# Attention and quantized feed-forward on one core: a new list of work (24 steps written out, the loop, the last eight), results summed into x, the norm as (x + minus) * rstd

## The chip, the cores and the metric

The kernel runs on 1 core of a Trainium2 chip. Its engines work side by side, each from a queue of its own, in order: TensorE (PE, with its weight loads shown as PEld), VectorE (DVE), ScalarE (ACT), GpSimd (POOL) and SyncE (SP), which here issues every DMA. The metric is the device time in microseconds (us); lower is better.

## The reference, cut to what matters

`x` has 4 batches of 2048 rows of 512 numbers, so 64 tiles of 128 rows.

```
x = x + (attention(layernorm(x), context) @ Wout + bout)
h = layernorm(x) * gamma + beta
h = qlinear(h, w1, b1)        # 512 -> 2048
h = gelu(h)
x = x + qlinear(h, w2, b2)    # 2048 -> 512

def qlinear(x, w, b):
    scale_x = 127 / max(abs(x), per row);  xq = round(x * scale_x)
    scale_w = 1 / mean(abs(w));            wq = clip(round(w * scale_w), -1, 1)
    return xq @ wq.T / (scale_x * scale_w) + b
```

The attention's mask lets query i see key j only where j mod 2048 equals i. A batch has 154 keys, so each of the first 154 queries of a batch sees one key and the result is that key's value row; every other query sees no key, all its scores are equal, and the result is the mean of the value rows. So the attention is a table of rows per batch: 128 rows (`front`), a tile of 26 rows and 102 times the mean (`second`), and the mean (`mean`), each multiplied by Wv and Wout.

## The kernel before, in words

The whole kernel is one list of short words, which `do` turns into instructions in exactly that order (`manual_schedule`). Each engine's queue is the part of the list that it executes; nothing else orders the work. `BEGINNING` is written out for the setup and steps U0 to U11, `STEADY` holds four steps with relative numbers and is repeated for rows 12 to 55, and `ENDING` holds the last eight. A step begins with `U`, the up product of row tile n. `n` counts row tiles in the order of `seq`, which puts a batch's first two tiles last.

Setup: `lv`, `lo` load Wv and Wout, `w` multiplies one block of them on TensorE (eight blocks, L415); `lw` loads a 1024-wide chunk of w1 (`lw0`) or w2 (`lw1`) into a buffer of the pool `ring`; `ms` sums its absolute values (L228 on DVE, L234 on ACT); `z0`, `z1` make the weight's scale (three parts: DVE, a small TensorE product of the tile `tot` at L206, DVE); `q` rounds the chunk (L217, L219) and `c` clips it (L222). `lc` loads the context, `lr0` to `lr3` load bout, gamma, beta and b2, `lb` half of b1. `pm`, `pr`, `Y` are TensorE products (L444) for the mean, the second tiles and the front tiles of a batch; `sr` writes the rows of the second tiles to DRAM, and `s`, `t` spread them from there with DMAs (`s`: L493 for 26 rows and L496 for the mean row repeated over 102 partitions; `t`: L499).

For each row tile: `L` loads a pair of tiles of x into a `ring` buffer. `a` (POOL) or `A` (DVE) adds the attention row (L246). `S` (DVE) takes mean and variance (L253). `N` (POOL, eight small instructions, L269 to L276), or `O`, `o`, `C` for the first four groups, makes rstd of a group of one to four tiles. The normed tile h is made by `k` (POOL, L306) or `n` (ACT, L299), followed by `e` (POOL: times gamma L311, plus beta L312); or by `P` and `E` on DVE alone (L320: (x - mean) * gamma; L325: times rstd, plus beta). `R` (DVE, L334) takes the largest value of a row; the group's last `R` makes the scale; `V` (POOL) or `v` (DVE) makes two more scales of the group. `Q` (ACT, L354) rounds h into 16-bit numbers and `T` transposes them by DMA (L365) into xqT, the operand of `U`. `X` (POOL) or `x` (DVE) adds b2 to x (L328).

`I n.half.v` seeds one half of the up product's PSUM tile with b1 times a scale (v = 1: DVE L524, v = 0: ACT L526). There are three such halves for all steps. `U` (16 products, L534) adds to it. `G` (ACT, L553) is the gelu of a half, `M` (DVE, L565) its largest value, the second `M` also makes the scale; `H` (ACT, L594) rounds the hidden row, `h` transposes it by DMA (L605) into hqT, and `W` (16 products, L612) is the down product into one of two PSUM tiles. `D` (POOL, L587) makes its scale, `F` (DVE, L618) computes x plus the scaled product into a tile `o` of two buffers, and `f` stores it (L623).

In the loop, `W` runs two steps behind `U`, loads run 14 to 16 tiles ahead, and behind the groups of rows that start at 12, 28 and 44 an `s`, behind the one that starts at 24 a `t` is inserted.

Of the kernel before, what the change touches and what calls it, by code (L numbers as in the profile page):

```python
# [37 lines left out]
F32 = mybir.dt.float32  # L38
I16 = mybir.dt.int16
# [14 lines left out]
def xattn_ffn(ctx: ExitStack, tc, x, ctxT, WvT, Wout, bout, w1T, b1, w2T, b2, gamma, beta, out):  # L54
# [22 lines left out]
    for g, size in enumerate(sizes):  # L77
# [4 lines left out]
    FIRST = 12  # L82
    BEGINNING = """
        lv0 lo0 lo1 lo2 lv1 lw0.2 lw0.3 lw0.6 lv2 w0 lw0.0 lv3 lv4 lo3 ms0.2.1 lo4 w1
        ms0.3.0 lw0.7 ms0.6.0 lw0.1 lo5 w2 ms0.0.1 lv5 lw0.4 lo6 lw0.5 lv6 w3 ms0.7.0 lo7
        ms0.1.1 lv7 lc w4 lw1.4 ms0.4.0 lw1.6 L0 ms0.5.0 lr0 w5 lr1 z0.0 lw1.2 z0.1 w6
        z0.2 q0.0.1 q0.5.0 q0.2.1 lw1.0 q0.7.0 lw1.5 sk2 c0.2.0 L1 sk3 c0.5.0 q0.4.0 sk1
        w7 lw1.3 ms1.4.0 sk0 c0.4.0 lw1.7 c0.7.0 cw0.1 q0.1.0 sf c0.0.0 cw1.0 lw1.1 pm0.2
        lr2 cw3.1 cw2.0 lk q0.3.0 c0.1.1 mk pm2.4 xo1 ms1.6.0 L2 q0.6.1 c0.6.1 L3 ms1.2.0
        Y0.0.2 m lb0 A0 a1 ms1.5.0 S0 Y0.2.4 ms1.0.0 O0 P0 o0 a2 ms1.3.0 C0 pr0.2 S1  # L90
        ms1.7.0 a3 O1 y0 ms1.1.0 c0.3.0 S2 o1 E0 a5 z1.0 R0 z1.1 z1.2 Q0 O2 Y3.0.2 P1 o2
        q1.6.0 T0 a6 C2 q1.2.0 L4 C1 lb1 V0 lr3 q1.0.0 E1 c1.2.0 Y3.2.4 R1 I0.0.0 P2 V1
        q1.3.0 pr2.4 a4 y3 S3 Q1 a8 I0.1.0 T1
        U0 O3 S4 L5 L6 c1.6.0 q1.7.0 S5 o3 E2 end G0.0 c1.0.0 C3 I1.0.0 R2 a7 I1.1.0
        U1 M0.0 V2 Q2 N4 P3 G0.1 c1.3.1 E3 q1.5.0 Y2.0.2 yr k4 q1.4.0 R3 k5 sr L7 e4 T2
        q1.1.0 Y2.2.4 S6 I2.0.1 G1.0 Y1.0.2 c1.1.0 G1.1 S7 M0.1 V3 I2.1.0 a10
        U2 I3.0.0 a13 M1.0 Q3 H0 M1.1 e5 T3 L8 s0 Y1.2.4 R4 G2.0 h0 N6 P6 L9 H1 A9 c1.7.1
        c1.5.1 R5 X0 I3.1.0
        U3 h1 t1 y1 G2.1 V4 M2.0 k7 I4.0.0 X3 S13 Q4 c1.4.0 W0 M2.1 G3.0 T4 a12 L10 G3.1
        S8 a11 Q5 y2 I4.1.0 T5 a14 M3.0  # L100
        U4 I5.0.0 e7 S9 H2 M3.1 W1 N8 G4.0 E6 h2 A15 G4.1 R6 R7 D0 I5.1.0 X1
        U5 M4.0 H3 D1 k8 F0 X4 S10 n9 D2 V6 Q6 S11 e8 W2 I6.0.0 T6 F1 h3 M4.1 G5.0 f0
        I6.1.0 X2 S12
        U6 H4 e9 S14 R8 Q7 M5.0 G5.1 T7 X5 R9 W3 f1 h4 G6.0 D3 N10 I7.0.1 Q8 A19 I7.1.0 T8
        M5.1 L11 V8 Q9
        U7 k10 G6.1 T9 a16 F2 n11 I8.0.1 f2 e10 H5 F3 W4 M6.0 G7.0 h5 a20 S16 n12 a17 M6.1
        I8.1.0
        U8 e11 G7.1 M7.0 I9.0.0 R10 H6 e12 R11 W5 M7.1 G8.0 h6 f3 D6 x7 D7 I9.1.0 D5 a18
        R12
        U9 H7 S15 D4 X6 F4 Q10 S17 a21 G8.1 T10 M8.0 W6 f4 V10 h7 G9.0 X10 S20 I10.0.0  # L110
        M8.1 N13 I10.1.0
        U10 S18 H8 k13 F5 k15 M9.0 X8 G9.1 h8 F6 e13 W7 Q11 S19 Q12 T11 M9.1 f5 G10.0 L12
        T12 N16 I11.0.0 f6 A22 W8 H9 x9 S21 a23 M10.0 I11.1.0 h9 D9 e15 S22 G10.1
        U11 F7 I12.0.0 M10.1 f7 D8 G11.0 k14 e14 W9 M11.0 H10 F8 k16 R13 I12.1.0 h10 e16
        R14 G11.1 R15 n17 M11.1 n18 e17 Q13 R16 H11 T13 F9 f8 V13 R17 f9 D10 X11 h11 t2
        e18
    """
# [21 lines left out]
    ring = ctx.enter_context(tc.tile_pool(name="ring", bufs=12))  # L139
# [99 lines left out]
    stats, rstd, shift, scale1, deq1, inv1 = {}, {}, {}, {}, {}, {}  # L239
# [24 lines left out]
    def row_norms(g):  # L264
# [3 lines left out]
        shift[g] = small.tile([P, 4], F32, tag="shift", name=f"shift_{g}")[:, :size]  # L268
# [353 lines left out]
    def store(n):  # L622
        nc.sync.dma_start(out=out_tiles[:, seq[n], :], in_=rows_out.pop(n))  # L623
# [131 lines left out]
```

## Time and profile before

| | |
|---|---|
| median of 3 runs | 524.63 us (524.53 to 524.99) |
| the profiled execution | 525.17 us, span 523.2 us |
| PE, DVE, ACT, POOL busy | 501.1, 433.2, 426.3, 410.5 us |
| DMA queue of SyncE | 93.56 MB, 75.1% of 16 engines |

A line of a timeline gives start, duration, engine, line, operation, output <- inputs and count, and in brackets the engine's idle time ahead of it and what ended it. A line of the groups gives count, then busy us and mean ns of one, then the idle time before the group. "x16" beside a product counts TensorE instructions; consecutive products overlap, so the distance from start to start (3.453 us for a `U` or a `W`) is the time they take. "PEclk" is the granted TensorE clock in tenths. In SyncE's timeline a DMA's duration is the time that the issuing took, not the transfer.

### The profile page before, as it was taken

To read this page: it belongs to the slowest core of one execution; us is meant where nothing else is said; L and a number is where in the kernel's file an instruction comes from. 1 tells how busy PE (TensorE), PEld (TensorE's weight loads), DVE (VectorE), ACT (ScalarE), POOL (GpSimd) and SP (SyncE) were. 2 spreads that over 40 slices of the span, in tenths; PEclk is the share of its full clock that TensorE was granted. 3 is DMA by queue.
4 is the path that set the end of the run, shared out by engine and by line. 5 is a ranking of instruction groups with operands and counts; after the bars stand their busy time and mean duration, and the time that the engine had idled before them with its cause. 6 is when DMAs were issued, how large, how long until landed. Compare 5 with 4: busy or idle time off the path is not lost.

```text
span 523.2 us, 6893 instructions
## 1 busy us (share of the span) xinstructions
PE 501.1 (96%) x2168; PEld 223.8 (43%) x2168; DVE 433.2 (83%) x753; ACT 426.3 (81%) x393; POOL 410.5 (78%) x532
## 2 busy tenths in 40 slices
PE   8997987999999989999999989999999899999996
PEld 3443432444444434444444434444444344444442
DVE  0188999889799889899999988999999888787762
ACT  2278987999788879888888878888889798888971
POOL 0048999999999999899999898999999998852220
PEclk9997998999999999999999999999999999999999
DMA  8998569376979695858697987679586956575664
GB/s 289 399 391 306 188 132 200 84 178 137 195 161 221 141 199 139 201 137 201 149 205 160 178 183 180 164 164 198 133 203 128 201 112 147 110 166 132 135 112 125
DMA packets 194112, 94.00 MB, mean 180 GB/s; under 512 B 170268, under 2 KB 170268, under 8 KB 194076
## 3 DMA queue, kind: packets, MB, share of 16 engines
q1 hardware_dynamic: 194076, 93.56, 75.1%
q8 instruction: 17, 0.28, 0.2%
q14 instruction: 19, 0.16, 0.1%
HBM read 34.55 MB, written 17.04 MB: 99 GB/s over the span
## 4 chain that ended last, share of the span: by engine, by line
PE 57%; POOL 18%; DMA 10%; DVE 6%; ACT 4%; issue 3%; SPq 1%; DVEq 0%; ACTq 0%; POOLq 0%
PE ph L534 27%; PE po L612 26%; DMA xqT<-xqg 6%; PE wps L415 4%; POOL x L246 4%; POOL h L312 3%; POOL h L311 3%; DVE m L565 2%; POOL x L328 2%; DMA x<-x_dram 2%; ACT hq L594 2%; DMA wv<-WvT_dram 2%; POOL h L306 1%; POOL r L270 1%; ACT hid L553 1%
## 5 line engine op out<-in xcount | busy, mean ns | idle before, releaser
L534 PE MATMUL ph<-w1q,xqT 128*128 128x512 f16 x1024 | 233.4, 381 | 10.1 <-DMA xqT<-xqg 7.8
L612 PE MATMUL po<-w2q,hqT 128*128 128x512 f16 x1024 | 231.3, 379 | 1.9 <-DMA hqT<-hq 1.2
L565 DVE TENSOR_REDUCE m<-hid 128x1 f32<-128x1024 f32 (+1 forms) x130 | 153.1, 1192 | 27.0 <-ACT hid L553 26.6
L553 ACT ACTIVATE hid<-ph,d 128x1024 f32<-128x1024 f32 (+1 forms) x130 | 140.9, 1095 | 31.4 <-PE ph L534 30.1
L534 PEld LDWEIGHTS <-xqT 128*128 128x128 f16 x1024 | 100.0, 98 | 135.2 <-DMA xqT<-xqg 12.1
L612 PEld LDWEIGHTS <-hqT 128*128 128x128 f16 x1024 | 100.0, 98 | 123.4 <-DMA hqT<-hq 2.2
L594 ACT ACTIVATE hq<-hid,i 128x2048 f16<-128x2048 f32 (+1 forms) x65 | 128.2, 1974 | 28.3 <-ACT ph L526 10.2
L526 ACT ACTIVATE ph<-b_b,inv 128x1024 f32<-128x1024 f32 x86 | 95.3, 1112 | 3.2 <-POOL inv L348 2.1
L312 POOL TENSOR_TENSOR h<-h,beta_b 128x512 f32<-128x512 f32 x59 | 75.6, 1282 | 4.6
L311 POOL TENSOR_TENSOR h<-h,gamma_b 128x512 f32<-128x512 f32 x59 | 75.0, 1271 | 3.9
L328 POOL TENSOR_TENSOR x<-x,b_b 128x512 f32<-128x512 f32 x61 | 77.0, 1272 | 0.0
L246 POOL TENSOR_TENSOR x<-x,mean 128x512 f32<-128x512 f32 x52 | 65.7, 1273 | 5.0 <-DVE mean L661 3.8
L618 DVE SCALAR_TENSOR_TENSOR o<-po,d,x 128x512 f32<-128x512 f32 x64 | 47.8, 746 | 16.0 <-PE po L612 10.6
L524 DVE TENSOR_SCALAR ph<-b_b,inv 128x1024 f32<-128x1024 f32 x42 | 53.2, 1267 | 0.6 <-ACT hid L553 0.6
L334 DVE TENSOR_REDUCE m<-h 128x1 f32<-128x512 f32 x64 | 42.9, 673 | 5.0 <-POOL h L312 5.0
L354 ACT ACTIVATE xqg<-h,s 128x512 f16<-128x512 f32 x64 | 45.4, 712 | 1.6 <-DVE s L342 1.6
L587 POOL TENSOR_TENSOR d<-mh,wm 128x1 f32<-128x1 f32 x64 | 12.5, 206 | 41.2 <-DVE mh L580 37.4
L253 DVE BATCH_NORM_STATS2 bn<-x 128x6 f32<-128x512 f32 x64 | 43.4, 679 | 0.6 <-POOL x L246 0.6
L306 POOL TENSOR_SCALAR h<-x,rstd,shift 128x512 f32<-128x512 f32 x54 | 41.9, 776 | 0.2
L415 PE MATMUL wps<-wo,wv 128*128 128x512 f32 x64 | 28.1, 595 | 1.5 <-DMA wv<-WvT_dram 1.5
L222 POOL TENSOR_SCALAR w1q<-wi 128x1024 f16<-128x1024 int16 x6 | 6.3, 1070 | 27.7 <-DVE wi L217 27.5
L415 PEld LDWEIGHTS wps<-wo,wv 128*128 128x128 f32 x64 | 11.9, 190 | 17.3 <-issue 13.9
(76 smaller groups left out, 261.3 us busy)
## 6 DMA issues: line engine op xcount, KB each, us to landing
x<-x_dram SPq DMA_DIRECT2D x32, 512.0 KB, 4.2
out_dram<-o SPq DMA_DIRECT2D x64, 256.0 KB, 2.8
ws<-w1T_dram SPq DMA_DIRECT2D x8, 512.0 KB, 7.2
ws<-w2T_dram SPq DMA_DIRECT2D x8, 512.0 KB, 9.6
wv<-WvT_dram SPq DMA_DIRECT2D x8, 256.0 KB, 8.5
wo<-Wout_dram SPq DMA_DIRECT2D x8, 256.0 KB, 4.5
ctx_sb<-ctxT_dram SPq DMA_DIRECT2D x1, 1232.0 KB
hqT<-hq SPq DMA_TRANSPOSE x65, 4.3
```

The lines of the kernel that those rows point to most:

```text
L246: e.tensor_tensor(x_of(n), x_of(n), y, ALU.add)
L311: nc.gpsimd.tensor_tensor(normed[n], normed[n], gamma_b, ALU.mult)
L312: nc.gpsimd.tensor_tensor(normed[n], normed[n], beta_b, ALU.add)
L328: e.tensor_tensor(x_of(n), x_of(n), b2_b, ALU.add)
L415: nc.tensor.matmul(wps[k // 2][:, (k % 2) * 512 : (k % 2 + 1) * 512], wv[c][:, k * P : (k + 1) * P], wo[c], start=(c == 0), stop=(c == KI ...
L524: nc.vector.tensor_scalar(ph, row, d, None, ALU.mult)
L526: nc.scalar.activation(ph, row, AF.Identity, bias=0.0, scale=d)
L534: nc.tensor.matmul(bank[i], xqT[n][:, k, :], w1q[:, k, i * 512 : (i + 1) * 512], start=False, stop=(k == KD - 1), skip_group_check=True,)
L553: nc.scalar.activation(hidden[n][:, i * w : (i + 1) * w], up_ps[n][half][:, lo : lo + w], AF.Gelu, bias=0.0, scale=deq1[g][:, j : j + 1],)
L565: nc.vector.tensor_reduce(m2[:, i : i + 1], hidden[n][:, i * w : (i + 1) * w], AX.X, ALU.max, apply_absolute_value=True,)
L594: nc.scalar.activation(hq[n][:, lo : lo + w], hidden[n][:, lo : lo + w], AF.Identity, bias=0.0, scale=inv2[n],)
L612: nc.tensor.matmul(po, hqT[n][:, k, :], w2q[:, k, :], start=(k == 0), stop=(k == KH - 1))
```

## The change

The list is replaced as a whole: `BEGINNING` now runs to step U23, the loop covers rows 24 to 55, and the last eight have another order. Words of each kind, before and after: `e` 59, 50; `k` 54, 50; `n` 5, none; `g` (new) none, 7; `P` 5, 14; `E` 5, 7; `X` 61, 59; `x` 3, 5; `V` 9, 12; `v` 12, 9; seeds on DVE 42, 37 and on ACT 86, 91; `ms` on DVE 3, 7 and on ACT 13, 9; `q` on DVE 3, 2 and on ACT 13, 14. All other counts stay, loads, transposes, stores, products and the four `s` and three `t` among them.

`F` writes its result over x, and `f` stores it from there, so tile `o` is gone and `ring` has 13 buffers for 12. `N` makes `minus` = -mean in place of `shift` = -mean * rstd, one instruction less. `k` computes (x + minus) * rstd. The new word `g` ends what `P` began on POOL: times rstd, plus beta.

```diff
-    FIRST = 12
+    FIRST = 24
...
+        lv0 lo0 lo1 lv1 lw0.5 lv2 lo2 lw0.7 lw0.3 w0 lw0.0 lo3 lo4 lv3 lw0.6 lv4 lw0.1 w1
+        lw0.4 ms0.0.0 lw0.2 lv5 ms0.7.0 lw1.5 lo5 w2 ms0.6.0 lc lo6 ms0.1.1 lv6 w3 ms0.3.1
+        lv7 ms0.4.1 lw1.7 L0 ms0.2.1 w4 lo7 ms0.5.1 lw1.2 z0.0 z0.1 w5 z0.2 ms1.5.1 q0.5.0
+        lr1 lw1.3 q0.3.0 sk1 lr0 q0.6.1 lw1.1 q0.0.0 c0.3.0 sk3 w6 sk2 L1 c0.5.0 q0.1.0
+        sk0 lw1.0 ms1.7.0 c0.1.1 mk lw1.6 sf q0.4.1 q0.2.0 w7 lw1.4 c0.2.1 L2 c0.4.1
+        q0.7.0 lr2 cw0.0 c0.7.0 L3 cw1.0 c0.0.0 pm0.2 cw2.1 ms1.2.0 lb0 lk xo0 cw3.1 pm2.4
+        ms1.1.1 lb1 c0.6.0 ms1.0.0 Y0.0.2 m A0 a1 ms1.6.0 S0 Y0.2.4 O0 ms1.4.0 P0 o0 a2 S1
+        ms1.3.0 C0 a3 S2 E0 a5 z1.0 R0 z1.1 z1.2 Q0 a6 O1 pr0.2 y0 q1.5.0 T0 V0 P2 lr3 L4
+        o1 I0.0.0 P1 L5 a7 C1 I0.1.0 O2 E1
+        U0 q1.1.0 o2 a4 S3 q1.4.0 O3 R1 c1.1.0 q1.6.0 S4 o3 q1.0.0 V1 c1.5.1 Y3.0.2 C2 X0
+        Q1 C3 end G0.0 T1 a9 pr2.4 S5 L6 I1.0.0 c1.6.1 N4 P3 q1.2.0 Y3.2.4 E2 I1.1.0 yr
+        U1 k5 R2 q1.3.0 E3 V2 G0.1 k4 M0.0 G1.0 a8 y3 Y1.0.2 I2.0.0 R3 c1.2.0 Q2 M0.1 e5
+        Y1.2.4 G1.1 T2 sr Q3 S8 Y2.0.2 I2.1.0 T3 S6 e4 y1 q1.7.0
+        U2 M1.0 H0 V3 R4 c1.7.0 S7 G2.0 h0 c1.3.0 R5 t1 Y2.2.4 I3.0.0 M1.1 c1.4.0 I3.1.0
+        c1.0.0
+        U3 S9 Q4 V4 N6 P6 H1 T4 A12 A11 G2.1 h1 W0 x3 N8 L7 E6 I4.0.0 L8 A10 G3.0 y2 k7
+        M2.0 I4.1.0
...
+        U16 k23 I17.0.1 X14 h14 G16.0 M15.1 f7 D14 X13 W13 G16.1 e23 F12 Q18 M16.0 I17.1.0
+        T18 s1 R20 L15 H15 D13 k21 M16.1 f8
...
     STEADY = """
-        U0 G0.0 I1.0.1 M0.0 W-2 G0.1 I1.1.0 M0.1 Q2 F-2 L14 f-2 D-1
-        U1 S11 H0 I2.0.1 G1.0 R6 T2 h0 G1.1 Q3 M1.0 X0 X1 I2.1.0 N8 W-1 k7 e7 T3 M1.1 F-1
-        k8 e8 H1 D0 a14 f-1
-        U2 I3.0.1 G2.0 h1 R7 M2.0 G2.1 Q4 M2.1 I3.1.0 W0 a12 L16 D2 D1 a13 R8 F0 T4 v4 S12
-        H2 h2
-        U3 X2 G3.0 I4.0.0 G3.1 S13 k9 e9 I4.1.0 W1 Q5 T5 a15 X3 M3.0 f0 M3.1 H3 k10 e10 h3
-        R9 F1 f1 S14
+        U0 W-2 G0.0 I1.0.1 G0.1 M0.0 Q2 k7 I1.1.0 T2 M0.1
+        U1 L14 e7 L16 G1.0 X0 H0 M1.0 W-1 a13 I2.0.1 Q3 h0 D-1 S11 G1.1 a15 T3 R6 I2.1.0
+        U2 N8 M1.1 G2.0 F-2 D0 R7 D1 a14 H1 W0 v4 I3.0.1 k9 G2.1 h1 X3 M2.0 I3.1.0 a12 F-1
+        U3 Q4 M2.1 e9 I4.0.0 T4 S12 H2 F0 k8 W1 S13 X1 G3.0 h2 G3.1 M3.0 e8 I4.1.0 M3.1 Q5
+        k10 T5 S14 H3 e10 f-2 f-1 F1 f0 R8 h3 R9 f1 X2 D2
...
-    ring = ctx.enter_context(tc.tile_pool(name="ring", bufs=12))
+    ring = ctx.enter_context(tc.tile_pool(name="ring", bufs=13))
...
-        e.tensor_tensor(q, stats[g][:, :size, 0], rstd[g], ALU.mult)
-        e.tensor_scalar(shift[g], q, -1.0, 0.0, ALU.mult, ALU.add)
+        minus[g] = small.tile([P, 4], F32, tag="minus", name=f"minus_{g}")[:, :size]
+        e.tensor_scalar(minus[g], stats[g][:, :size, 0], -1.0, 0.0, ALU.mult, ALU.add)
...
     def normalize(n):
         g, j = group_of[n]
         h = normed[n] = hp.tile([P, D], F32, tag="h", name=f"h_{n}")
-        nc.scalar.activation(
-            h, x_of(n), AF.Identity, bias=shift[g][:, j : j + 1], scale=rstd[g][:, j : j + 1]
-        )
...
+        m, r = minus[g][:, j : j + 1], rstd[g][:, j : j + 1]
+        nc.gpsimd.tensor_scalar(h, x_of(n), m, r, ALU.add, ALU.mult)
...
+    def half_affine(n):
+        g, j = group_of[n]
+        h, r = normed[n], rstd[g][:, j : j + 1]
+        nc.gpsimd.tensor_scalar(h, h, r, 1.0, ALU.mult, ALU.mult)
+        nc.gpsimd.tensor_tensor(h, h, beta_b, ALU.add)
...
     def finish(n):
-        rows_out[n] = tile([P, D], F32, "o", n)
-        nc.vector.scalar_tensor_tensor(
-            rows_out[n], down_ps.pop(n), deq2[n], x_of(n), ALU.mult, ALU.add
-        )
+        t = x_of(n)
+        nc.vector.scalar_tensor_tensor(t, down_ps.pop(n), deq2[n], t, ALU.mult, ALU.add)
...
     def store(n):
-        nc.sync.dma_start(out=out_tiles[:, seq[n], :], in_=rows_out.pop(n))
+        nc.sync.dma_start(out=out_tiles[:, seq[n], :], in_=x_of(n))
...
-        "n": normalize,
-        "k": normalize_too,
+        "k": normalize,
...
+        "g": half_affine,
```

## The prediction

> **What bounds the kernel now.** I read the page's busy times and clock first, then TensorE's timeline for every gap, then for each gap the wait and the queue that ended it, and last the busy time by stage.
>
> ```profile
> PE 501.1 (96%) x2168; PEld 223.8 (43%) x2168; DVE 433.2 (83%) x753; ACT 426.3 (81%) x393; POOL 410.5 (78%) x532
> ...
> PEclk9997998999999999999999999999999999999999
> ```
>
> TensorE (PE) is the bound: 64 rows of up and down product, each 3.453 us from start to start, are 442.0 us that nothing here changes. What can move is the time in which it stands. TensorE's timeline shows where:
>
> ```profile
> 54.55 3.62 PE L534 MATMUL ph<-w1q,xqT 128*128 128x512 f16 x16
> ...
> 76.03 1.89 PE L534 MATMUL ph<-w1q,xqT 128*128 128x512 f16 x8 [1.57 <-ACT ph L526]
> 78.88 1.90 PE L612 MATMUL po<-w2q,hqT 128*128 128x512 f16 x8 [0.96 <-DMA hqT<-hq]
> 81.44 1.89 PE L612 MATMUL po<-w2q,hqT 128*128 128x512 f16 x8 [0.67 <-POOL w2q L222]
> 85.72 5.31 PE L534 MATMUL ph<-w1q,xqT 128*128 128x512 f16 x16 [2.39 <-DMA xqT<-xqg]
> ...
> 190.10 3.63 PE L534 MATMUL ph<-w1q,xqT 128*128 128x512 f16 x16 [2.06 <-DMA xqT<-xqg]
> ```
>
> Step U0 starts at 54.55. Behind it lie 442.0 us of rows and 6.9 us of attention rows (12 products in 5.15, 4 in 1.8), so TensorE could end at 503.5; it ends at 519.3. The 15.8 us lost divide by place. **Start, U0 to U5** (54.55 to 94.32): 39.8 us for 31.1 of work, 8.7 lost, 1.7 of it because U4 (at 85.72) ran at the slow clock. **Middle, U5 to U18** (at 190.10): 95.8 for 93.2, 2.5 lost. **From U18**: 4.6 lost, nearly all in three gaps before U30, U34 and U50 (0.6, 1.5, 1.8 by starts).
>
> The gaps from U18 on have one cause, which SyncE's timeline shows:
>
> ```profile
> 179.48 1.07 SPq L623 DMA_DIRECT2D out_dram<-o  x1
> 180.61 0.41 SPq L493 DMA_DIRECT2D second<-rest_dram  x1
> 181.07 0.32 SPq L496 DMA_DIRECT2D second<-rest_dram  x1
> 181.49 0.40 SPq L176 DMA_DIRECT2D x<-x_dram  x1
> 183.01 0.36 SPq L623 DMA_DIRECT2D out_dram<-o  x1
> 183.48 1.70 SPq L365 DMA_TRANSPOSE xqT<-xqg  x1
> ```
>
> The transpose T18 is issued behind the spread of attention rows (words s, t), a load of x and a store, and takes 6.6 us to land where a transpose of the hidden rows takes 4.3 (page, median). In loops without s or t the same queue costs nothing.
>
> The stages say how full the other engines are when TensorE has no gap (columns: window, length, busy us of PE, PEld, DVE, ACT, POOL):
>
> ```profile
> 100.00:150.00 50.00, 50.00 (x233) 22.63 (x232) 42.78 (x79) 45.82 (x42) 47.02 (x68) 1.00 0.73 161
> 150.00:190.00 40.00, 37.90 (x175) 16.83 (x173) 36.60 (x62) 34.89 (x32) 37.77 (x53) 1.00 0.85 186
> ...
> 310.00:400.00 90.00, 90.00 (x419) 40.83 (x417) 84.11 (x140) 78.72 (x69) 84.21 (x102) 1.00 0.74 165
> ```
>
> From 100 to 190 POOL is at 94% and DVE at 88%; from 310 to 400 both run at 93.5% and TensorE does not wait. I use 93.5% as the fullness that is still free.
>
> **The change, part by part.** The sum is made against the profiled execution's 525.17 us, 0.54 above the median of 524.63.
>
> *Work per engine.* Prices are these rows:
>
> ```profile
> L312 POOL TENSOR_TENSOR h<-h,beta_b 128x512 f32<-128x512 f32 x59 | 75.6, 1282 | 4.6
> L311 POOL TENSOR_TENSOR h<-h,gamma_b 128x512 f32<-128x512 f32 x59 | 75.0, 1271 | 3.9
> L306 POOL TENSOR_SCALAR h<-x,rstd,shift 128x512 f32<-128x512 f32 x54 | 41.9, 776 | 0.2
> L320 DVE SCALAR_TENSOR_TENSOR h<-x,mv,gamma_b 128x512 f32<-128x512 f32 x5 | 5.0, 1003 | 0.0
> ```
>
> POOL: 9 fewer e (2.55 each) -23.0; 4 fewer k -3.1; 7 new g (0.776 + 1.282) +14.4; 2 fewer X (1.272) -2.5; each of 17 N one 0.2 us instruction shorter -3.4; 3 more V (0.38) +1.1. Sum -16.5. ACT: 5 n gone (0.804) -4.0, 4 measures gone (1.24) -5.0, 1 q more +1.1, 5 more seeds (1.112) +5.6: -2.3. DVE: 9 more P +9.0, 2 E (0.92) and 2 x (0.88) +3.6, 4 measures +4.9, 1 q (0.75) fewer, 5 seeds (1.267) fewer -6.3, 3 v (1.58) fewer -4.7: +5.8, of which +1.6 outside the start. None of this is on the path by itself; it decides stalls in the start and the middle.
>
> The new form of k has the same shape and engine as L306 and is priced the same. Sums into x (F writes x, the store reads x, no tile o): the o tile's one wait, 4.7 us of DVE on a store at about 108, ended beside gapless TensorE, so nothing is gained. What it adds is that a pair of x is free only after its stores; the load that needs the slot comes 13 pairs later, so the 13th buffer covers it. Without cover a load waits one store, 2.8 us.
>
> *Start, before U0.* Weight chunks land at a steady rate: the first of w1 is measured at 9.30, the eighth at 23.95, with 5.5 MB between, 0.375 MB/us. The new list has all eight after 6.5 MB instead of 7.25 (22.0 instead of 24.0), but five of them are now measured one behind another on DVE (1.22 each, from 19.3): the scale is ready at 25.2, as before (25.13). In TensorE's queue the scale's product moves from behind block w5 to behind w4, which is done by about 23: it now waits some 2.2 us with w5 to w7 queued behind it, and w3 waits 1.1 for lv3 (4.25 MB, 16.0). The attention product ends at about 36.7, not 33.9. Row 0 needs beta too, at 15.45 MB, 45.8 (before 44.8), so most of this is hidden: T0 goes out at about 48.5 (before 47.4) and U0 starts at about 52, where before it waited for front rows until 54.55. But 5.2 us of those front rows (Y3, half of pr) now lie behind U0. Net +2.6. Bounds: U0 at 50 (+0.6) if T0 lands as fast as before, at 54 (+4.6) if both waits grow.
>
> *Start, U0 to U5.* The front rows between the steps give POOL (30 us of work for steps 0 to 3), DVE (28) and ACT (29) 29 us of TensorE time instead of 24; so I expect the four gaps of 0.67 to 2.39 and the 0.5 before U1 to close but for 1.4 (bounds 1.0 and 3.9, half of what is lost at full clock and a little more). TensorE however idles about 2.7 us before U0. A pause of 3.2 us at 42.5 was followed by products at half pace (46.77: 6.23 us for 3.45 of work, 2.8 lost), and U4 behind gaps of 0.67 and 2.39 lost 1.7; the 2.06 before U18 lost none. So the price lies between 0 and 2.8; a pause of 2.7 lies between the first two: 2.1. Loss 3.5 instead of 8.7: -5.2, bounds -7.7 and -2.0.
>
> The Trainium skill, "TensorE: Matmul & The Clock Gate", Part 1, says that the clock halves after a whole idle window of about 3.4 us. The trace halves it behind shorter gaps. By the page the pause before U0 would be free and the sum 2.1 us lower.
>
> *Middle, U5 to U18.* T18 stands ahead of s1 in the new list, so the 2.2 us gap goes. What comes is fuller DVE. P took 0.74 us when POOL was quiet and 1.67 when POOL was in a tensor-tensor; 13 more such instructions cost between 9.6 and 21.7, against 11.0 of seeds and v that leave: DVE moves by -1.4 to +10.7. I take the mean rows (+1.6), which leave DVE near 90%, under the free 93.5%, and 2.0 us of stalls for unevenness: 2.0 instead of 2.5, -0.5.
>
> The Trainium skill, "GPSIMD Engine Reference", Specifications, says GpSimd shares its SBUF interfaces with VectorE and contends with instructions of two SBUF inputs: a rule against this part. By it nearly all 13 pay the upper price, and the sum is that of rival 3.
>
> *From U18.* The loop's work is equal. Q2 and T2 come earlier, so no load or store stands between s and T2; but L14 and L16 now go out together between T2 and h0, and stores f-2, f-1, f0 together ahead of h3. h0 is issued about 12 us after U0 and has until 17.3; its landing today is 4.0 to 4.3 us, so some 1 us is spare. With s ahead I expect 1.7 us lost for each of s2 and s3 (today 1.5 and 1.8), 0.2 for t3, 0.1 in each of eight loops, 0.3 at the end (unchanged): 4.5 to 4.6, as before: 0. Bounds: -3.5 (no loop gap) and +8 (1 us in each loop).
>
> **Sum:** +2.6 - 5.2 - 0.5 + 0 = -3.1: 522.1 profiled, 521.5 as a median.
>
> **Rivals.** 1. *It works throughout*: U0 at 50, no slow clock, middle and loop without gaps: +0.6 - 7.7 - 2.5 - 3.5 = -13.1, 511.5; with half of the extra over my forecast, 516.5. For it: every closed gap is a queue order, and order is what changes. Against: the pause before U0. 2. *No change*: the slow clock at 2.8 and gaps of 2.1 instead of 1.4 in the start, loops at 0.3: -3.1 + 1.4 + 1.6 = -0.1, 524.5. For it: both are inside the bounds above; against: it needs both at once. 3. *Slower, DVE becomes the bound*: 13 two-input instructions at 1.67 add 10.7 us to DVE between U3 and U23; its 11.3 us of idle time from 94 to 188 shrink to 0.6, and at 93.5% it needs 6.1: TensorE waits 5.5 us more in the middle and the sum turns to +2.4, 527.0. The sum changes sign at about 1.5 us a piece. Against: four of the five P were shorter than that.
>
> **How the numbers follow.** Forecast (518.5 to 523.5) 0.42; rival 1 (below 518.5) 0.23; rival 2 0.10; rival 3 0.25. 0.2% (1 us) is what a measurement here tells from no change. Faster 0.65, same 0.10, slower 0.25. The range reaches half-way into rival 1's best and past rival 3: 513.5 to 529.0.
>
> **What would show it.** TensorE's timeline: U0 near 52 with a wait in front and products above 3.62 us behind it; a wait on the tot row before w5; gaps before U4 and U18 gone; gaps of 1 to 2 us after s2 and s3. POOL near 394 us busy. Wrong if L320's mean passes 1.5 us and DVE's waits end TensorE's gaps, or if hqT gaps return in each loop.

## The result, and the profile after

The changed kernel takes 522.04 us (median of 20 runs, 520.63 to 525.11) for 524.64 before (20 runs beside it, 523.78 to 527.47): a ratio of 0.9957, 95% interval 0.9943 to 0.9970, so 2.6 us faster. The profiled execution took 520.9 us with a span of 519.1, near the fast end of its runs; against the profile of before (525.17, span 523.2) it gains 4.1 us of span and 4.3 of time, so some 1.7 us of what follows belongs to those two executions.

The page of the changed kernel: busy times, the granted clock in 40 slices, and the shares of the chain that ended last.

```profile
PE 500.0 (96%) x2168; PEld 222.2 (43%) x2168; DVE 425.0 (82%) x757; ACT 420.4 (81%) x386; POOL 395.8 (76%) x512
...
PEclk9998999999999999999999999999999999999999
...
PE 68%; DMA 18%; DVE 8%; ACT 2%; POOL 1%; issue 1%; SPq 0%; ACTq 0%; POOLq 0%; DVEq 0%
```

POOL lost 14.7 us of busy time and with it its place in the chain: before, 18% of the chain was POOL and 57% TensorE. DVE, which was to grow by 5.8, fell by 8.2. TensorE's timeline of the changed kernel shows where it still stands:

```profile
25.57 0.38 PE L229 MATMUL pt<-tot,ones 128*128 128x1 f32 x2 [2.08 <-DVE tot L226]
...
47.55 0.38 PE L229 MATMUL pt<-tot,ones 128*128 128x1 f32 x2 [3.24 <-DVE tot L226]
48.73 3.65 PE L465 MATMUL py_rest<-w_sb,ctx_rest 128*128 128x512 f32 x4 [0.80 <-DVE wm L232]
53.01 3.20 PE L555 MATMUL ph<-w1q,xqT 128*128 128x512 f16 x14 [0.63 <-DMA xqT<-xqg]
...
250.15 3.63 PE L633 MATMUL po<-w2q,hqT 128*128 128x512 f16 x16 [0.41 <-DMA hqT<-hq]
...
272.60 3.63 PE L633 MATMUL po<-w2q,hqT 128*128 128x512 f16 x16 [1.56 <-DMA hqT<-hq]
```

U0 starts at 53.01 for 54.55, with 5.2 us more of attention rows behind it. From there to U18 (179.00) TensorE does 33 rows of 3.453 and 28 attention products of 0.43, 126.0 us, in 126.0: **nothing is lost where 11.2 us were lost before**. The gaps before U4 and U18 are gone. From U18 to the start of the last `W` (511.50) lie 94 rows, 324.6 us, in 332.5: **7.9 lost, where before 93 rows, 321.2, took 325.5: 4.4 lost**. In the forecast's split, which counts to the end, that is 8.1 for 4.6. So the parts are +3.6 before U0 (with the attention rows that moved behind it), -8.7 from U0 to U5, -2.5 from there to U18, +3.5 from U18: -4.1.

TensorE's waits, with total, number and longest, show the same exchange; before, the largest was 7.8 us in five waits on xqT:

```profile
PE pt L229 <- DVE tot L226: 5.3, 2, 3.2
PE po L633 <- DMA hqT<-hq: 5.2, 10, 1.6
...
PE ph L555 <- DMA xqT<-xqg: 0.6, 1, 0.6
```

What is late now are transposed hidden rows (hqT). Take the gap at 250.15, the `W1` of its group. ScalarE, VectorE and SyncE of the changed kernel ahead of it:

```profile
241.06 1.11 ACT L574 ACTIVATE hid<-ph,d 128x1024 f32<-128x1024 f32 x1 [1.33 <-issue]
242.07 1.99 ACT L615 ACTIVATE hq<-hid,i 128x2048 f16<-128x2048 f32 x1
```

```profile
240.64 0.16 DVE L603 RECIPROCAL i<-mh 128x1 f32<-128x1 f32 x1
```

```profile
244.09 1.78 SPq L626 DMA_TRANSPOSE hqT<-hq  x1
```

The scale of the row is ready at 240.8, ScalarE is idle, and yet the rounding H1 (L615) starts at 242.07: the gelu G2.0 stands ahead of it in the list and starts at 241.06. (The profile names no releaser for it; it reads the first half of the `U` begun at 239.08, 1.98 us earlier, and the `G` at 234.10, which the profile has waiting for TensorE, also started 1.92 us behind its `U`.) h1 is issued at 244.09, its `W` could have started at 249.74, and h1 lands at 250.15. The old list has H1 ahead of G2.0.

The room of a transpose, from its issue to the moment its `W` is due (3.453 us behind the start of the product ahead of it), tells the two loops apart. Over the eight groups from row 24 on, h0 had 7.6 to 8.8 us before and has 5.4 in every group now; h1 had 8.4 to 8.8 and has 5.35 to 5.9 in all but one. The median time from issue to landing is 4.3 us before and 4.4 now, so the old loop had room for a late transpose and the new one has little. The largest gap, 272.60, is h0 behind t3, as SyncE's timeline shows:

```profile
261.95 0.40 SPq L520 DMA_DIRECT2D mean<-rest_dram  x1
262.45 1.19 SPq L386 DMA_TRANSPOSE xqT<-xqg  x1
263.69 1.08 SPq L199 DMA_DIRECT2D x<-x_dram  x2
265.48 4.17 SPq L626 DMA_TRANSPOSE hqT<-hq  x1
```

Behind the spread t3, a transpose and the loads L14 and L16, the issue of h0 alone takes 4.17 us (1.8 to 2.0 for an h1 or h2, with no load or store directly ahead), and it lands 7.1 us after it was begun. In the other groups with loads ahead of h0 its issue takes 1.8 to 3.0 us, except in two, where the load had ended only 0.4 and 0.5 us before: 3.8 and 4.0 us, and these two have a gap before `W0` as well (0.5 each by starts).

Last, the groups that the rival of the slower side rested on:

```profile
L341 DVE SCALAR_TENSOR_TENSOR h<-x,mv,gamma_b 128x512 f32<-128x512 f32 x14 | 10.6, 769 | 0.0
L346 DVE SCALAR_TENSOR_TENSOR h<-h,rstd,beta_b 128x512 f32<-128x512 f32 x7 | 7.0, 1006 | 0.4 <-POOL rstd L296 0.4
...
L323 POOL TENSOR_SCALAR h<-x,minus,rstd 128x512 f32<-128x512 f32 x50 | 38.4, 768 | 0.4
```

`P` costs 0.77 us, not the 1.5 at which the sign would have changed, and the new form of `k` costs what the old one did (0.776). The stage from 100 to 150, with the columns of the prediction's table, shows that fuller engines cost nothing:

```profile
100.00:150.00 50.00, 50.00 (x233) 22.69 (x232) 47.65 (x87) 47.21 (x44) 47.87 (x69) 1.00 0.74 176
```

DVE at 95% and POOL at 96% are above the 93.5% that the forecast took as free, and TensorE still had no gap.

### The profile page after: what moved, and what is told of

It is laid out like the page before. It is cut to its first block, busy times and chain, and to the rows that moved or that the text cites. A ratio compares the mean times of both kernels' runs of the same rounds, so it can differ in the third digit from the quotient of the medians.

```text
span 519.1 us, 6893 instructions
## 1 busy us (share of the span) xinstructions
PE 500.0 (96%) x2168; PEld 222.2 (43%) x2168; DVE 425.0 (82%) x757; ACT 420.4 (81%) x386; POOL 395.8 (76%) x512
## 4 chain that ended last, share of the span: by engine, by line
PE 68%; DMA 18%; DVE 8%; ACT 2%; POOL 1%; issue 1%; SPq 0%; ACTq 0%; POOLq 0%; DVEq 0%
PE po L633 32%; PE ph L555 32%; DMA hqT<-hq 12%; DMA wo<-Wout_dram 3%; DVE m L586 2%; PE py L465 2%; DMA ws<-w2T_dram 2%; DVE ph L545 1%; ACT hid L574 1%; DVE m L355 1%; DMA wv<-WvT_dram 1%; POOL x L269 1%; DVE x L639 1%; DVE bn L276 1%; PE py_mean L465 1%
## 5 line engine op out<-in xcount | busy, mean ns | idle before, releaser
L615 ACT ACTIVATE hq<-hid,i 128x2048 f16<-128x2048 f32 (+1 forms) x65 | 128.0, 1970 | 18.5 <-DVE i L603 8.8
L547 ACT ACTIVATE ph<-b_b,inv 128x1024 f32<-128x1024 f32 x91 | 100.5, 1112 | 1.2 <-POOL inv L369 0.8
L349 POOL TENSOR_TENSOR x<-x,b_b 128x512 f32<-128x512 f32 x59 | 74.8, 1270 | 0.0
L269 POOL TENSOR_TENSOR x<-x,mean 128x512 f32<-128x512 f32 x51 | 65.1, 1280 | 11.2 <-DMA x<-x_dram 9.5
L327 POOL TENSOR_TENSOR h<-h,beta_b 128x512 f32<-128x512 f32 x50 | 63.8, 1275 | 3.9
L326 POOL TENSOR_TENSOR h<-h,gamma_b 128x512 f32<-128x512 f32 x50 | 63.5, 1270 | 1.8
L639 DVE SCALAR_TENSOR_TENSOR x<-po,d,x 128x512 f32<-128x512 f32 x64 | 47.1, 739 | 10.9 <-PE po L633 10.6
L545 DVE TENSOR_SCALAR ph<-b_b,inv 128x1024 f32<-128x1024 f32 x37 | 47.3, 1277 | 0.0
L323 POOL TENSOR_SCALAR h<-x,minus,rstd 128x512 f32<-128x512 f32 x50 | 38.4, 768 | 0.4
L251 DVE TENSOR_REDUCE part<-ws 128x1 f32<-128x1024 f32 x7 | 8.1, 1209 | 19.5 <-DMA ws<-w1T_dram 19.5
```

Of the source, the lines that this page charges most:

```text
L269: e.tensor_tensor(x_of(n), x_of(n), y, ALU.add)
L326: nc.gpsimd.tensor_tensor(normed[n], normed[n], gamma_b, ALU.mult)
L327: nc.gpsimd.tensor_tensor(normed[n], normed[n], beta_b, ALU.add)
L349: e.tensor_tensor(x_of(n), x_of(n), b2_b, ALU.add)
L545: nc.vector.tensor_scalar(ph, row, d, None, ALU.mult)
L547: nc.scalar.activation(ph, row, AF.Identity, bias=0.0, scale=d)
```

## The experiments

All ratios are against runs of the kernel before on the same chip. Experiments 1 to 4, 5 to 8 and 9 to 12 ran on three chips, on which the kernel before took 524.57, 524.57 and 524.70 us in the median. The last section of this part puts the profiles in one table.

### 1. The new start with the old loop and ending

```diff
 (changed kernel)
-    STEADY, ENDING of the change
+    STEADY, ENDING of before
```

> The changed kernel with the loop and the last eight steps of the kernel before; the written-out 24 steps, the sums into x and the norm stay new. Theory A (the start and the middle gain some 7.5 us, the new loop gives some 2 to 3 back): TensorE's waits on hqT behind U24 (10 of them, 5.2 us) go, and the waits on xqT after t3, s2 and s3 (0.6, 1.5, 1.8 us) come back: 520.0 us as a median, 2.0 under the changed kernel's 522.04. Rival B (the waits on hqT come from what the 24 steps hand over: engines that run later than before): they stay, 522 us. Rival C (the new loop is better, as its place in the change suggests): 524 us or more.

Measured: 518.30 us (6 runs), ratio 0.9887, 0.9866 to 0.9908: faster than both kernels, and 1.7 below what theory A expected. TensorE's waits on hqT fall from 5.2 us in ten to 1.4 in three, as it said. The start, with sums into x and the new norm, is worth 6.3 us; the new loop behind it takes 3.7 of them back. The loop's gaps are at the old places: by starts 0.35 us before U30 (behind t3), 1.6 before U34 (s2) and 1.0 before U50 (s3).

### 2. The old start with the new loop and ending

```diff
 (kernel before)
-    STEADY, ENDING of before
+    STEADY, ENDING of the change
```

> The kernel before with the new loop, run from row 12, and the new last eight. Theory A: the start keeps its 8.7 us of loss, and 11 rounds of the new loop lose about 0.5 each, and 1 to 2 more behind each s and t: 525 to 528 us, slower than before's 524.6. Rival C (the new loop is better): the losses from U18 on fall from 4.6 to under 2 us, 521 to 523 us.

Measured: 605.01 us, ratio 1.1529; the expectation missed by 77 us. VectorE's waits in this kernel:

```profile
DVE o L616 <- DMA out_dram<-o: 99.2, 12, 9.3
```

The new loop issues f-2, f-1 and f0 together, behind T5. With two buffers of tile o, `F` must wait for the first of these stores, and everything behind `F` on VectorE waits too. Sums into x, costed at nothing, are what makes this loop possible. Experiment 8 repeats it with them.

### 3. Sums into x and the 13th buffer alone, on the kernel before

```diff
-        rows_out[n] = tile([P, D], F32, "o", n)
-        nc.vector.scalar_tensor_tensor(
-            rows_out[n], down_ps.pop(n), deq2[n], x_of(n), ALU.mult, ALU.add
-        )
+        t = x_of(n)
+        nc.vector.scalar_tensor_tensor(t, down_ps.pop(n), deq2[n], t, ALU.mult, ALU.add)
...
-    ring = ctx.enter_context(tc.tile_pool(name="ring", bufs=12))
+    ring = ctx.enter_context(tc.tile_pool(name="ring", bufs=13))
```

> The kernel before, where F writes over x, the store reads x, and ring has 13 buffers. Theory A: the one wait on a store (4.7 us of VectorE at 108) goes without effect on TensorE: 524.6 us, within 0.5. Rival D (the o tile's two buffers held results, psum and so TensorE up in places): 1 to 3 us faster.

Measured: 526.19 us (10 runs), ratio 1.0023, 1.0007 to 1.0039. No gain, as forecast, and rather a loss of 1.2 us (0.4 to 2.0); the trace shows no wait that it could be put down to (11.2 us lost from U0 to U18 and 4.5 behind it, as before), so where it lies stays open.

### 4. TensorE's pauses of the new start filled with products

```diff
 (changed kernel; di: two idle products; rest_sum does its first half twice)
-        ... z0.0 z0.1 w5 ...
+        ... z0.0 di z0.1 w5 ...
-        ... m A0 a1 ms1.6.0 S0 Y0.2.4 O0 ...
+        ... m A0 a1 ms1.6.0 S0 Y0.2.4 Y0.0.2 Y0.2.4 O0 ...
```

> The changed kernel with products that change no result put into TensorE's pauses before the first and the second weight scale and before U0 (two of the size of the idle ones, the front rows of batch 0 a second time, half of the rest rows a second time). Theory E (the scatter of the changed kernel, 520.6 to 525.1 us with a mean clock of 0.997 down to 0.987, is the clock that falls behind pauses of 2 to 3 us ahead of U0): the slow stretches go, the scatter falls under 2 us and the median to 520.5. Rival F (the scatter is in the DMAs): median and scatter as before, 522 us, or 1 us more where the added products delay a scale.

Measured: 520.56 us (10 runs, 517.79 to 525.00), ratio 0.9922, 0.9893 to 0.9951. The five lower runs had granted clocks of 0.997 to 1.000 and took 517.8 to 519.5; but one at 1.000 took 521.63, so the clock is not all. The median is where theory E put it, but the scatter, which was to fall under 2 us, grew from 4.5 to 7.2. The profile contradicts the expected place of the gain: U0 starts at 54.97, 2.0 us *later* than without filling, and it is the loop that lost less, 4.6 us for 7.9, with the same list. The gaps before `W1` are gone in it. So the new loop's gaps come and go between executions; that h1 is issued only 5.4 us before its `W` is due makes this possible. The next experiment gives it more room.

### 5. One word of the new loop: H1 ahead of G2.0

```diff
 (changed kernel)
-        U2 N8 M1.1 G2.0 F-2 D0 R7 D1 a14 H1 W0 v4 ...
+        U2 N8 M1.1 H1 G2.0 F-2 D0 R7 D1 a14 W0 v4 ...
```

> The changed kernel with one word moved in the loop: the rounding H1 of the hidden row stands before the gelu G2.0 on ScalarE, not behind it. In the changed kernel's profile H1 starts at 242.07 although its scale was ready at 240.80, because G2.0 (241.06, 1.1 us) stands ahead; h1 is then issued 5.4 to 6 us before its W, which is about what it takes to land. Theory A (the new loop's own order makes h1 late): the three gaps before W1 of a group (0.57, 0.67 and 0.74 us by starts) go, and nothing else grows, since M2.0 is behind two scales on VectorE anyway: 520.0 against 522.0 for the changed kernel. Rival (those gaps come from how long a transpose takes to land, which differs from run to run, and G2.0 1.8 us later makes H2 late instead): no gain, 522.0 to 523.0.

Measured: 518.48 us (517.13 to 519.17), ratio 0.9882, 0.9868 to 0.9896; every run is faster than every run of the changed kernel. ScalarE and SyncE of this kernel in the same group as above:

```profile
241.74 2.00 ACT L615 ACTIVATE hq<-hid,i 128x2048 f16<-128x2048 f32 x1 [1.16 <-issue]
243.65 2.10 ACT L574 ACTIVATE hid<-ph,d 128x1024 f32<-128x1024 f32 x2
```

```profile
243.77 1.76 SPq L626 DMA_TRANSPOSE hqT<-hq  x1
```

This execution runs 0.85 us later at this place (its `U` of the step is at 239.94 for 239.08), so h1 goes out 1.2 us earlier than before the edit, and its `W` starts without a gap at 250.43. In seven of the eight groups h1 has 6.5 to 6.7 us of room, for 5.35 to 5.9 before the edit. No gap before any `W1` is left; what is left in the loop is 2.2 us behind t3 and 0.35 before W27. Theory A holds: 3.6 us by the medians, which is more than the three gaps that the expectation counted (2.0). The loss from U18 on (4.5 for 7.9) agrees, but by itself shows less, since the profile of experiment 4 lost as little with the order of the change.

### 6. The second load of a group moved behind h0

```diff
 (changed kernel)
-        U1 L14 e7 L16 G1.0 ...
+        U1 L14 e7 G1.0 ...
-        U2 ... D1 a14 H1 W0 v4 ...
+        U2 ... D1 a14 H1 L16 W0 v4 ...
```

> The changed kernel with the second load of a group (L16) moved from beside L14, ahead of h0, to just behind h1's rounding, ahead of h1. Theory A (two loads together ahead of h0 make it late): the gap behind t3 (1.7 us) shrinks by the 0.4 to 1.1 us that one load takes in the queue and on the engines, the two gaps of 0.5 before W0 go, h1 is not later because its load is issued before its operand is ready: 520.7 against 522.0. Rival (h1 has even less room than h0): the gaps before W1 grow by about 0.5 us in each of eight groups, 524 to 526.

Measured: 520.50 us (520.12 to 521.44), ratio 0.9925, 0.9913 to 0.9938; 1.5 faster than the changed kernel. SyncE's and TensorE's timelines of this kernel behind t3:

```profile
263.48 0.57 SPq L199 DMA_DIRECT2D x<-x_dram  x1
266.44 2.03 SPq L626 DMA_TRANSPOSE hqT<-hq  x1
268.57 1.55 SPq L386 DMA_TRANSPOSE xqT<-xqg  x1
270.17 0.58 SPq L199 DMA_DIRECT2D x<-x_dram  x1
273.39 1.76 SPq L626 DMA_TRANSPOSE hqT<-hq  x1
```

```profile
271.84 3.62 PE L633 MATMUL po<-w2q,hqT 128*128 128x512 f16 x16
275.30 3.62 PE L555 MATMUL ph<-w1q,xqT 128*128 128x512 f16 x16
279.46 2.76 PE L633 MATMUL po<-w2q,hqT 128*128 128x512 f16 x12 [0.55 <-DMA hqT<-hq]
```

With one load ahead of it, and 2.4 us between them for 0.7, h0 is issued in 2.03 us for 4.17. The gap behind t3 is gone (271.84), and so are the two other gaps before a `W0`. What remains is a gap before `W1` (279.46) in each of the eight groups, 0.3 to 0.8 by starts: h1's lateness by itself. Both theories saw a part: theory A the median (520.7), the rival the gaps before `W1`. The profile, of the slowest of the five runs, lost 7.7 us from U18 on, hardly less than the changed kernel's 7.9, so the 1.5 us rest on the medians.

### 7. The spread of the mean row cut, on the kernel of experiment 1

```diff
-        nc.sync.dma_start(out=second[b][REST:, :], in_=row.partition_broadcast(P - REST))
+        nc.sync.dma_start(out=second[b][REST:32, :], in_=row.partition_broadcast(32 - REST))
+        nc.sync.dma_start(out=second[b][32:, :], in_=row.partition_broadcast(P - 32))
```

> The first experiment's kernel (new start, old loop; 518.3) with the spread of the mean row over 102 partitions cut into 6 and 96 partitions. In the trace of before the DMA engines fall to 20 to 30% busy for some 2 us behind that transfer. The Trainium skill, 'DMA: Bandwidth & Descriptors', section 'Why a DMA increments its semaphore by 16 and not by 1', says that a transfer is split over the largest count up to 16 that divides its partitions: 6 engines for 102, 16 for 96. Theory D (the spread is late because few engines carry it): of the gaps behind s (0.93 and 0.58 behind s1, 1.60 behind s2, 1.04 behind s3) half goes, 516.3. Rival (what delays the next transpose is only its place behind these transfers in the queue): one issue of 0.35 us more per spread, 518.3 to 519.0.

Measured: 516.18 us (515.09 to 516.63), ratio 0.9839, 0.9825 to 0.9852: 2.1 faster than experiment 1. TensorE behind s3, first without the cut (experiment 1), then with it:

```profile
403.63 2.97 PE L635 MATMUL po<-w2q,hqT 128*128 128x512 f16 x13
407.48 3.63 PE L557 MATMUL ph<-w1q,xqT 128*128 128x512 f16 x16 [0.87 <-DMA xqT<-xqg]
```

```profile
402.24 3.62 PE L636 MATMUL po<-w2q,hqT 128*128 128x512 f16 x16
405.69 3.62 PE L558 MATMUL ph<-w1q,xqT 128*128 128x512 f16 x16
```

The gaps behind s2 (1.6 by starts) and s3 (1.0) are gone; those behind s1 are not. The two transposes behind s2 are issued in 1.29 and 3.18 us for 2.09 and 4.42, those behind s3 in 1.29 and 3.35 for 1.42 and 4.56. One more DMA in the queue made the transposes behind it faster, so it was the transfer over 102 partitions and not the queue's order alone. The number of engines that the Trainium skill gives ("DMA: Bandwidth & Descriptors", "Why a DMA increments its semaphore by 16 and not by 1") is in accord with this, but no run here counts the engines of one transfer.

### 8. Old start, sums into x, new loop

```diff
 (experiment 3)
-    STEADY, ENDING of before
+    STEADY, ENDING of the change
```

> The kernel before with sums written into x, 13 buffers (as in the third experiment, 526.2) and the changed kernel's loop and ending; its start and middle are those of before. It is the second experiment without tile o, whose two buffers held up the late stores there. Theory A (the new loop by itself costs 3.4 us more than the old, 8.0 lost from U18 on for 4.6): 526.2 plus 3.4, 529.6. Rival (the new loop suffers only from the state in which the new start leaves the engines, or its gaps in that profile were of that one execution): 525.5 to 527.0. If stores still stop VectorE, it is above 535 and the waits of the finish show it.

Measured: 524.86 us (11 runs), ratio 1.0008, 0.9996 to 1.0020, so 1.3 *less* than experiment 3, not 3.4 more, and below the rival's range too. Without tile o the 99 us of experiment 2 are gone. In the profile the new loop still loses more from U18 on (5.8 us for 4.5), with gaps before `W1` and one of 2.2 behind t3; what it gains are the gap before U18, since here it runs from row 12 and sends T ahead of s1 (10.2 lost from U0 to U18 for 11.2), and 1.3 before U0, where the two lists do not differ. So the gaps of the new loop appear behind the old start as well, but here the kernel as a whole pays nothing for it; the 3.7 us of experiment 1 hold behind the new start, and the 1.3 of loss here are of one execution of each kernel.

### 9 to 12. Put together

9: both loop edits (H1 early, L16 behind h0); 10: with the cut spread too; 11: experiment 7 with the filling of experiment 4; 12: experiment 10 with s1 later.

```diff
 (9: changed kernel)
-        U1 L14 e7 L16 G1.0 ...
-        U2 N8 M1.1 G2.0 F-2 D0 R7 D1 a14 H1 W0 v4 ...
+        U1 L14 e7 G1.0 ...
+        U2 N8 M1.1 H1 G2.0 F-2 D0 R7 D1 a14 L16 W0 v4 ...
 (12: in BEGINNING)
-        T18 s1 R20 L15 H15 D13 k21 M16.1 f8
-        U17 f9 e21 f10 h15 G17.0 ...
+        T18 R20 L15 H15 D13 k21 M16.1 f8
+        U17 f9 e21 f10 h15 s1 G17.0 ...
```

> The changed kernel with both loop edits at once: H1 ahead of G2.0 (518.48 alone) and L16 ahead of h1 and not of h0 (520.50 alone). With H1 early alone, one large gap was left in the loop, 2.2 us behind t3; with L16 moved alone, that gap was gone but one of 0.5 to 0.8 stood before W1 in each of eight groups. Theory A (two separate causes, each taken away by its own edit): no gap in the loop, 518.5 minus 2.2, 516.3. Rival (they trade: with L16 ahead of h1, H1 early is used up): 518.0 to 519.0, with gaps of 0.2 to 0.4 before W1 back.

Measured: 517.16 us (516.66 to 520.31), ratio 0.9867, 0.9844 to 0.9890. The edits add up in part: 1.3 less than H1 early alone, for 2.2 expected. The largest waits left in the loop are of 0.7 us, behind t3 (273.41) and at 364.79. SyncE behind t3 shows how the first comes about:

```profile
265.59 0.57 SPq L199 DMA_DIRECT2D x<-x_dram  x1
266.79 3.89 SPq L626 DMA_TRANSPOSE hqT<-hq  x1
...
272.03 0.58 SPq L199 DMA_DIRECT2D x<-x_dram  x1
272.72 3.33 SPq L626 DMA_TRANSPOSE hqT<-hq  x1
```

One load 0.1 to 0.6 us ahead makes the issue of h0 and h1 nearly as long as two did. What counted in experiment 6 was thus not only the number of the loads but how near they stood.

> The same, with the spread over 102 partitions cut into 6 and 96 partitions as in the seventh experiment. In the old loop the cut was worth 2.1 us (518.3 to 516.18), of which the trace shows the gaps behind s2 and s3 gone (1.60 and 1.04) and those behind s1 not (0.83 and 1.06 for 0.93 and 0.58). The new loop has no gap behind s2 and s3, since Q2 and T2 come earlier, and the same s1. So theory D expects nothing here: 516.3, as without the cut. Rival (the cut also frees DMA engines for what is in flight): 515.0 to 515.8.

Measured: 517.13 us, ratio 0.9858, 0.9841 to 0.9876: no gain over experiment 9, as theory D said, though 0.8 above its 516.3; the new loop sends Q2 and T2 so early that the slow spread hurts nothing.

> The seventh experiment's kernel (new start, old loop, cut spread; 516.18) with the products of the fourth experiment that fill TensorE's pauses before z0.1, z1.1 and U0. Theory E (what the filling gained there, 522.04 to 520.56, is the slow clock behind the pauses): the same gain, 514.0 to 515.0, and a granted clock of 0.997 in most runs. Rival (the profile of the fourth experiment has U0 2.0 us later than the changed kernel's, and lost 4.6 us from U18 on where the changed kernel's lost 7.9; so the gain was gaps of the new loop that went, and the clock gave nothing): the old loop has no such gaps, and the later U0 is paid in full: 517.5 to 518.2.

Measured: 515.06 us (514.35 to 517.16), ratio 0.9813, 0.9800 to 0.9827: the fastest kernel of the study, 9.6 us below before and 7.0 below the changed kernel. The rival is refuted; theory E is right in sign, with 1.1 us for the 1.2 to 2.2 it expected. Four of five runs had a granted clock of 0.999 to 1.000 (without filling 0.990 to 0.996) and took 514.4 to 515.6. The profile is of the fifth (0.996, 517.16): U0 at 54.91, 2.1 later, and a half clock before U0 in spite of the filling (TensorE was busy for 1.59 of the 3.42 us ahead of it; the last section has what this means). How the runs at full clock are laid out no trace shows.

> The tenth experiment's kernel with s1 moved in the written list from behind T18 to behind h15. In all kernels with the new start, h15's W waits 0.5 to 0.9 us, and the W after the next as long, because h15 is issued behind s1, a load and three stores. Theory (the place of s1 in the queue is the cause): both gaps go, 1.3 us less than the tenth, 515.0. Rival (three stores and a load ahead of h15 are enough; or T19, now behind s1, is late): no gain, 516.3 to 517.

Measured: 516.83 us, ratio 0.9853, 0.9839 to 0.9867: 0.3 below experiment 10, not 1.3. Yet both gaps went, but for 0.2 before 191.34: TensorE of this kernel, first at U0, then behind s1.

```profile
52.95 5.44 PE L556 MATMUL ph<-w1q,xqT 128*128 128x512 f16 x16 [0.89 <-DMA xqT<-xqg]
...
180.75 3.62 PE L556 MATMUL ph<-w1q,xqT 128*128 128x512 f16 x16
184.21 3.62 PE L634 MATMUL po<-w2q,hqT 128*128 128x512 f16 x16
187.66 3.62 PE L556 MATMUL ph<-w1q,xqT 128*128 128x512 f16 x16
191.34 3.63 PE L634 MATMUL po<-w2q,hqT 128*128 128x512 f16 x16
```

The loss from U18 on is 2.1 us, the smallest of all. Part of it was given back before: U0's products took 5.44 us for 3.62, and the granted clock of all its runs was 0.989 to 0.990, with a start that is word for word that of experiment 10 (three of four runs at 0.997). The one run of experiment 10 at 0.990, its profiled one, took 518.74, and the four here 516.41 to 518.12: at one clock the edit is worth more than 0.3, but a single run does not say how much.

### All profiles in one table

Loss is time from start to start less 3.453 us a row and 0.43 an attention product: from U0 to U18 (126.0 us of work with the new start, 124.3 with the old), and from U18 to the last `W` (94 rows, or 93). Times in the last column are those of the profiled executions.

| kernel | U0 | lost U0 to U18 | lost from U18 | profiled, us |
|---|---|---|---|---|
| before | 54.55 | 11.2 | 4.4 | 525.17 |
| changed | 53.01 | 0.0 | 7.9 | 520.90 |
| 1 new start, old loop | 52.47 | 0.0 | 5.0 | 517.60 |
| 2 old start, new loop | 55.38 | 17.0 | 76.7 | 605.00 |
| 3 sums into x | 55.09 | 11.2 | 4.5 | 526.22 |
| 4 pauses filled | 54.97 | 0.0 | 4.6 | 519.49 |
| 5 H1 early | 52.91 | 1.0 | 4.5 | 518.36 |
| 6 loads apart | 52.98 | 0.2 | 7.7 | 521.44 |
| 7 old loop, spread cut | 52.78 | 0.0 | 3.0 | 515.80 |
| 8 old start, sums, new loop | 53.78 | 10.2 | 5.8 | 524.91 |
| 9 H1 early, loads apart | 54.31 | 0.3 | 5.2 | 520.31 |
| 10 the same, spread cut | 53.34 | 0.3 | 5.2 | 518.74 |
| 11 as 7, filled | 54.91 | 0.0 | 2.3 | 517.16 |
| 12 as 10, s1 late | 52.95 | 1.8 | 2.1 | 516.74 |

## Why the prediction was right, point by point

The time (521.5 for 522.04), the range and the sign hold. The parts do not hold as well: two errors of about 2.5 and 2.0 us in the start and the middle were paid for by one of 3.5 in the loop, and the median moved 1.7 less than the profile. That the total came out within 0.5 us is in good part luck.

**Work per engine**: right for POOL (394 forecast, 395.8). For DVE +5.8 was forecast and -8.2 measured; the 14 `P` took 10.6 us where 5 had taken 5.0, so 5.6 for the 9.0 forecast, and the small instructions of `v` and of the scales became shorter: `v` fell from 19.0 us for twelve to 9.1 for nine, -9.9 for -4.7. Rival 3, DVE as the bound through 13 two-input instructions, is refuted by the 0.77 us of L341. The Trainium skill's rule on shared interfaces ("GPSIMD Engine Reference", Specifications), weighed there, spoke for the upper price, and the traces do not contradict it. Ten of the 14 `P` ran beside no 128x512 tensor-tensor of POOL and took 0.72 to 0.75 us; four ran beside one for 0.16 to 0.46 us and took 0.75 to 0.97. In the kernel before, two ran beside one for 0.58 and 1.59 us and took 1.13 and 1.67. So the price stayed low because the new list has `P` mostly where POOL does something else. The prediction did not look at that, and took the mean of `P` before for its sum.

**Sums into x at nothing**: right as an edit by itself (experiment 3: no gain, and a loss of about 1 us that is not explained). What the step lacked is that the new loop cannot do without it: 605 us (experiment 2). Its reading of the one wait on a store was wrong in place: in the trace of before those 4.7 us end at 517.49, ahead of the last `F` but one, and not at about 108. The last `F` waits for the last `W` all the same (519.36), so the sum is not touched.

**Start, before U0**: the mechanism was right. The wait of the scale's product was 2.08 (2.2 forecast), U0 at 53.01 (52). The term is +3.6 for +2.6, inside its bounds. What it mis-sized is the pause: 3.24 us before z1.1, not 2.7 before U0, and the slow clock fell on the half rest rows behind it (3.65 us for 1.8), ahead of U0.

**Start, U0 to U5**: the sign was right, the size too small: -8.7 for -5.2, outside the bounds of -7.7. All gaps closed, not all but 1.4 us. The 2.1 for a slow clock at U0 was taken from neighbouring pauses; in eight profiles of the new start without filling, what was lost behind U0 was 0 to 1.8 us, and 0 in the changed kernel's. By the Trainium skill ("TensorE: Matmul & The Clock Gate", Part 1) a pause of 2.7 us there was to be free; the pause before U0 was of 0.63 us, so the changed kernel does not test it. The clock halved behind pauses of 3.24 and 0.80 us with a product of 0.38 between them, and in the kernel before behind one of 2.39 (ahead of U4), none of them a whole idle window of 3.4 us: here the measurement decides, and the last section gives what the traces show in its place.

**Middle**: T ahead of s1 closed the gap, as said; the 2.0 us kept for DVE's unevenness were 0.

**From U18**: the step that failed. "h0 is issued about 12 us after U0 and has until 17.3; its landing today is 4.0 to 4.3 us, so some 1 us is spare" looked at h0 alone, and "0.1 in each of eight loops" was a guess. The room of h0 was right (5.4 us); its landing was not, where a load stands close ahead of it (7.1 us behind t3). H1, moved behind G2.0 by the same diff, was not costed, and it leaves h1 5.35 to 5.9 us before its `W` is due, for 8.4 to 8.8 in the old loop: moving that word back gave 3.6 us. Of the named gaps, s2 and s3 were forecast at 1.7 each and are 0 and 0.5, t3 at 0.2 and is 1.7, through the loads close ahead of h0 (experiment 6). Total 0 forecast, +3.5 in the profile, inside the bounds of -3.5 to 8.

**Rival 1** ("every closed gap is a queue order") was the nearer truth for the start, and with the old loop it was nearly there: 518.3, with the cut spread 516.18.

## What to carry to other kernels

When a list is laid out anew, cost each consumer of the bound engine by its room: from the moment its transpose can be issued to the moment its product is due, and look at *every* word that stands ahead of it on each queue. A step with as much work as before can still lose 3.6 us by one word that waits for TensorE ahead of one that does not. Try the halves of such a change apart: here start and loop were of opposite sign, and the new start with the old loop beat both kernels.

## What the runs showed of the hardware

In the old loop a copy of one row to 102 partitions slows the transposes behind it; the same bytes as 6 and 96 partitions, with one DMA more, slow them less (2.1 us of the whole, experiment 7). In the new loop, which sends Q2 and T2 earlier, the cut gains nothing (experiment 10).

A transpose takes longer to issue close behind a load. In eight profiles with the new loop (changed, 4, 5, 6, 8, 9, 10, 12; from 200 us on) the transposes of hidden rows that began within 0.8 us of the end of a load's issue took 3.3 to 4.9 us to issue, in all sixteen cases, behind one load or two. With 2.5 us or more between them it was 1.7 to 2.0 in thirty of 31.

How long a transpose takes to land also differs between executions of the same list. In the changed kernel the h1 issued at 244.09 landed 6.1 us later, and its DMA engines were busy for 60.6% of the 8 us from 243 on to move 0.66 MB; in the profile of experiment 4, at the same step, h1 landed in 5.35 us or less, and it was 42.9%. Why is open.

The slow clock comes in steps. In each of the fourteen profiles the granted clock changes only at times that lie a multiple of 3.41 us apart, and between the first product at full clock and the last product a half-clock stretch is one or two such steps long. Windows cut at the steps, with the busy times of PE, PEld, DVE, ACT, POOL, then the granted clock; first the changed kernel, then experiment 12, whose lists are the same there:

```profile
45.40:48.81 3.41, 0.46 (x3) 0.41 (x4) 3.00 (x12) 1.18 (x3) 3.41 (x4) 1.00 0.96 383
48.81:52.22 3.41, 3.41 (x4) 0.99 (x4) 2.75 (x8) 3.33 (x4) 3.41 (x5) 0.50 0.33 59
```

```profile
46.41:49.83 3.42, 1.15 (x4) 0.79 (x5) 3.28 (x12) 0.94 (x2) 3.42 (x3) 1.00 0.55 223
49.83:53.24 3.41, 2.52 (x4) 0.46 (x3) 2.75 (x7) 3.33 (x4) 3.41 (x6) 0.50 0.47 81
53.24:56.65 3.41, 3.41 (x9) 1.21 (x8) 3.24 (x10) 3.11 (x4) 3.41 (x4) 0.50 0.88 288
```

Over all profiles, a step at full clock in which TensorE was busy for 1.35 us or less was followed by half clock every time, one with more than 1.6 never; of six between, three were. The gap of 2.39 us before U4 in the kernel before fell into a step with 1.03 us busy, the one of 2.06 before U18 into one with 1.74. At half clock, a step with up to 2.73 us busy was followed by another at half, one with 2.87 or more by full clock. So the same pause costs one step or two by where the steps happen to lie: in the changed kernel TensorE was busy all through the slow step, in experiment 12 the wait before U0 fell into it, and a second followed. Those 3.4 us more at half speed cost about 1.7 (an estimate, half of them), and 1.8 were lost behind U0. That is enough to hide what experiment 12 gained in the loop. What decides where the steps lie is open.
